# Block maxima of a softmax turned by VectorE in 32x32 blocks and gathered by ScalarE copies, in place of a TensorE transpose

## The chip, the cores and the metric

The kernel runs on one core of one Trainium2 chip. A core has five engines that run side by side and meet only through semaphores: TensorE (PE in the profile, with its weight loads as PEld), VectorE (DVE), ScalarE (ACT), GpSimd (POOL) and SyncE (SP, which only issues DMAs here). The metric is the device time of one execution in microseconds (us), lower is better; the number given for a kernel is the median of several executions.

## What is computed

Two transformer layers over x of 2 batches x 1024 tokens x 512 features, all in float32. In each layer attention and feed-forward both read the same normalised input:

```python
xn = _layernorm(x)
x = x + attention0(xn) + ffn0(xn)      # hidden size 2048
xn = _layernorm(x)
x = x + attention1(xn) + ffn1(xn)      # hidden size 1408, ternary weights with scales
```

Attention has 16 heads of 32 features, rotated queries and keys, and a causal softmax:

```python
scores = einsum('bhqd,bhkd->bhqk', q, k) * 32 ** -0.5
scores = where(causal, scores, lowest)
pattern = softmax(scores, axis=-1)
heads = einsum('bhqk,bhkd->bqhd', pattern, v)
```

The feed-forward part is `down(silu(gate(xn)) * up(xn))`.

## The kernel before, in words

**Stages.** There are four phases, one for each (layer, batch): layer 0 batch 0, layer 0 batch 1, layer 1 batch 0, layer 1 batch 1. In a phase the 16 heads are taken as 4 groups of 4 heads (`HG`), so that 4 heads of 32 features fill 128 partitions. In a group the 1024 queries are taken in 4 blocks of 256 (`QB`). One group and one query block make a `Run`; there are 4 x 4 x 4 = 64 of them. A run with query block `qb` has `qb + 1` steps, each over 256 keys, so a phase has 40 steps and the kernel 160.

**A run.** `scores(n)` computes transposed scores (keys on partitions, queries along the free dimension) with TensorE and lets ScalarE move them to SBUF tile `s`. `blocks(n, h2)` takes maxima with VectorE: a reduction with a built-in transpose gives, for blocks of 32 queries, the maximum over each block of 32 keys; these collect in `rmax`. After the last step one more reduction brings them to `m1`, a tile of 128 partitions x 32: partition 32a + p is query p of its block of 32 as seen by the a-th quarter of the key partitions, and the column is head and query block. What is still missing is the maximum over the four quarters a, which lie on different partitions. `maxima()` does this: it turns `m1`, so that the 32 columns become partitions, and reduces over a to `m2` (32 x 32). `m2` goes to DRAM (`md`), and `spread()` reads it back with a broadcast to all 128 partitions (`mb`). Then `subtract`, `exps`, `summed` (sums of exponentials, on GpSimd and VectorE) and `weighted` (product with the values on TensorE) follow; `weighted` of a step comes `LAG` = 5 steps after its scores.

**Filling.** Between the scores and the weighted sums of a step, TensorE gets other work: feed-forward products, projections, output products (`Fill.run` with its lists). Many of these are written as seven products of half-size blocks, whose results are called `ux`, `uy`, `uz`; `d` is the down product. Their results lie in three PSUM banks (`bank()`, pool `p_m`), which the transpose in `maxima()` uses too.

**Order.** The kernel is not written out in its final order. Every operation is recorded with estimated costs (`Schedule.record`), then a planner (`Schedule.again`) places it: TensorE's pieces keep nearly the recorded order, and each of the other engines takes, among what is ready, what is due first. Each engine then executes its instructions in the planned order, in order, and a waiting instruction holds what stands behind it on its engine. All recorded calls are issued through one helper line (278), so the profile's groups are told apart by tile names and not by lines.

**The place of the change.** When the last step of a run has been recorded (`n == run.steps - 1`), the run is put in the list `found`. `transpose_maxima()` is called before every piece of filling work; it records `maxima()` and `spread()` once the planner's clock says that `m1` is done, or at the latest at the end of the next step's filling, by `transpose_maxima(True)`. `spread_maxima` lets at most two runs hold an `mb` at a time (`rows[0] < 2`).

Of the kernel before, what the change touches and what calls it, by code (L numbers as in the profile page):

```python
# [11 lines left out]
F32 = mybir.dt.float32  # L12
AF = mybir.ActivationFunctionType
ALU = mybir.AluOpType
AX = mybir.AxisListType
# [3 lines left out]
P = 128  # L19
# [6 lines left out]
HG = P // DH  # L26
# [3 lines left out]
SQ = 32  # L30
NSQ = QB // SQ
# [12 lines left out]
def ts(n, size):  # L44
    return slice(n * size, (n + 1) * size)
# [460 lines left out]
def two_layers(ctx: ExitStack, tc: tile.TileContext, x_in, attn_w, ffn_w, ffn_s, rope, out):  # L506
    ctx.enter_context(tc.manual_schedule())
    nc = Schedule(tc.nc)

    def pool(name, bufs, space=None):  # L510
        real = ctx.enter_context(tc.tile_pool(name=name, bufs=bufs, **({"space": space} if space else {})))
        return Pool(real, bufs, {"p_m": "m", "p_av": "av"}.get(name, "other") if space is PSUM else None)
# [20 lines left out]
    small = pool("small", 2)  # L533
# [9 lines left out]
    def bank_free(n):  # L543
        return nc.settled(bank_last[n]) if bank_last[n] else 0.0

    def bank(name, shape=(P, TB), hold=False):
        nc.advance(nc.tensor.free)
        n = min((n for n in range(3) if not bank_held[n]), key=lambda n: (bank_free(n), bank_last[n].first.seq if bank_last[n] else 0))
        bank_held[n] = hold
        t = bank_last[n] = p_m.tile(list(shape), F32, tag=f"m{n}", name=name)  # L550
        if hold:
            bank_of[name] = n
        return t
# [4 lines left out]
    ident = fixed.tile([P, P], F32, tag="ident", name="ident")  # L558
# [633 lines left out]

    waiting, rows = [], [0]

    found = []

    def transpose_maxima(now=False):
        while found and (now or nc.settled(found[0].m1) <= nc.tensor.free):
            found.pop(0).maxima()
            spread_maxima()  # L1200

    def spread_maxima():
        while waiting and rows[0] < 2:
            rows[0] += 1
            waiting.pop(0).spread()

    class Run:
# [69 lines left out]

        def maxima(self):

            tr = bank(f"mtr{self.name}", (HG * NSQ, P))  # L1280
            nc.tensor.transpose(tr, self.m1.rearrange("p h b -> p (h b)"), ident)
            m2 = small.tile([HG * NSQ, SQ], F32, tag="m2", name=f"m2_{self.name}")
            nc.vector.tensor_reduce(m2, tr.rearrange("c (a p) -> c p a", p=SQ), AX.X, ALU.max)
            self.md = dram.tile([HG * NSQ, SQ], F32, tag="md", name=f"md{self.name}")
            nc.sync.dma_start(out=self.md, in_=m2)
            waiting.append(self)
# [124 lines left out]
    now = [0]  # L1411
# [4 lines left out]
    class Fill:  # L1416
# [111 lines left out]
        def run(self, step, share, between=()):  # L1528

            spent = 0.0  # L1530
            while True:

                n = next((i for i, item in enumerate(self.timed) if item[0] <= step), None)
                if n is not None:
                    self.timed.pop(n)[1]()
                    continue
                transpose_maxima()
                chosen = self.choose(step)
                if chosen is None:
                    return spent  # L1540
                fn, cost = chosen
                if spent + cost / 2 > share:
                    return spent
                spent += fn()
                if between:
                    between.pop(0)()
# [124 lines left out]
    def weight(i):  # L1671

        if i >= total + LAG - 6:
            return 1.5
        return 1.2 if i % per_phase < 10 else 1.0
# [3 lines left out]
    for i in range(total + LAG):  # L1679
        ph = min(i // per_phase, len(phases) - 1)  # L1680
        now[0] = i
        if i % per_phase == 0 and i < total:
            while ph not in marks:
                assert fill.run(i - 1, 5.0)
            queue_phase(ph)
        run, n = steps[i] if i < total else (None, 0)
        if run:
            while turned.get((ph, run.g)) != 4:
                assert fill.run(i - 1, 5.0)
            run.scores(n)  # L1690
            if ended and ended.acc:
                ended.total()
        old, m = steps[i - LAG] if i >= LAG else (None, 0)
        if run and n == run.steps - 1:
            run.mask(n)

        if ended:
            ended.normalise()
            ended = None

        def exponentials(r, k, h2, sums=True):
            r.subtract(k, h2)
            r.exps(k, h2)
            if sums:
                r.summed(k, h2)
            if h2 == 1:
                spread_maxima()

        def late(r, k):

            return k == 0 and r.steps == LAG - 1

        between = []
        if old and late(old, m):
            between += [lambda h2=h2: exponentials(old, m, h2) for h2 in range(2)]
        elif old and m == 0:
            for h2 in range(2):
                old.summed(0, h2)
        if run:
            between += [lambda h2=h2: run.blocks(n, h2) for h2 in range(2)]  # L1720
        if 0 <= i - LAG + 1 < total:
            r, k = steps[i - LAG + 1]
            if not late(r, k):

                between += [lambda h2=h2: exponentials(r, k, h2, k > 0) for h2 in range(2)]
        end = total + LAG if ph == len(phases) - 1 else (ph + 1) * per_phase
        share = fill.left((ph + 1) * per_phase) * weight(i) / sum(weight(j) for j in range(i, end))
        goal = share + max(-4.0, min(4.0, carried))
        spent = fill.run(i, goal, between)
        while between:  # L1730
            between.pop(0)()
        transpose_maxima(True)
        if run and n == run.steps - 1:
            found.append(run)
        carried = goal - spent
        if old:
            while (old.ph, 2 * m + 1) not in v:
                spent += fill.run(i, 5.0)
                carried = goal - spent
            tiles = [old.s[m]]  # L1740
            while i < total and spent - goal < 6.0 and max(nc.settled(t) for t in tiles) > nc.tensor.free + SOON:
                more = fill.run(i, 2.0)
                if not more:
                    break
                spent += more
                carried = goal - spent
            old.weighted(m)
            if m == old.steps - 1:
                ended = old

                nc.advance(nc.tensor.free)
                if i + 1 >= total or nc.settled(old.sums) <= nc.tensor.free:
                    old.total()
# [59 lines left out]
```

## Time and profile before

| quantity | value |
|---|---|
| time, median of 3 runs | 1811.73 us (1811.0 to 1814.87) |
| the profiled execution's own time | 1814.8 us |
| its span, first to last instruction | 1812.9 us |
| mean granted TensorE clock | 0.998 |
| PE busy, weight loads | 1798.0 us (99%), 880.0 us (49%) |
| DVE, ACT, POOL busy | 1476.3 (81%), 1041.7 (57%), 1232.6 us (68%) |
| instructions | 25807 |
| DMA | 165.15 MB, 28.5% of 16 engines' span |

Busy shares are averages over the whole span. In the tables of groups, a line gives engine, operation, out<-in by the program's tile names (digits at the end left out, so `m1` and `m2` both read `m`), the shape, how many, the busy time and the mean duration in ns; behind the bar stands the idle time of the engine just before these instructions, and what ended it. In the timeline the first two numbers are the start and the length in us. The end of a matmul is modelled, and the next one can start before it; so time on TensorE is read from start to start.

### The profile page before, as it was taken

The page shows a single profiled execution, that of the slowest core. Times are in us where ns is not written, and L with a number is a line of the kernel's source. Part 1 is how long each engine was busy: PE and PEld are TensorE (multiplying, and loading weights), DVE is VectorE, ACT ScalarE, POOL GpSimd, SP SyncE. Part 2 cuts the span into 40 slices and gives each one's busy share as a digit, 9 for nine tenths or more (in the row PEclk, how much of TensorE's full clock was granted, in tenths as well). Part 3 has the DMA queues.
Part 4 walks back from the last instruction along what each step waited for, and adds up shares of the span by engine and source line. Part 5 has one row for each costly group of instructions (what it writes and reads, how often), then busy time and mean ns, then how long its engine had stood idle before and what let it go on. Part 6 is the DMA issues. An engine that isn't in the chain of part 4 may idle for free.

```text
span 1812.9 us, 25807 instructions
## 1 busy us (share of the span) xinstructions
PE 1798.0 (99%) x9406; PEld 880.0 (49%) x9406; DVE 1476.3 (81%) x1975; ACT 1041.7 (57%) x1240; POOL 1232.6 (68%) x1145
## 2 busy tenths in 40 slices
PE   9999999999999999999999999999999999999998
PEld 5464444444444644444444455444444464444443
DVE  3665988868879668779697798888979998989988
ACT  2444665556546565554575556576565757565762
POOL 6726875956868337446377894886779775866775
PEclk9999999999999999999999999999999999999999
DMA  5324343222232422222133324222223322221211
GB/s 192 99 82 137 114 148 120 67 80 82 80 113 88 138 72 68 70 82 89 56 97 102 115 76 160 76 80 71 77 84 98 125 69 71 70 69 50 67 39 71
DMA packets 140334, 165.15 MB, mean 91 GB/s; under 512 B 13360, under 2 KB 93488, under 8 KB 140208
## 3 DMA queue, kind: packets, MB, share of 16 engines
q1 hardware_dynamic: 140208, 163.50, 28.5%
q8 instruction: 75, 1.23, 0.3%
q14 instruction: 51, 0.42, 0.1%
HBM read 134.62 MB, written 28.84 MB: 90 GB/s over the span
## 4 chain that ended last, share of the span: by engine, by line
PE 89%; POOL 5%; DVE 3%; issue 1%; ACT 1%; DMA 1%; SPq 0%; POOLq 0%; ACTq 0%; DVEq 0%
PE d L278 24%; PE ux L278 19%; PE uy L278 9%; PE sc L278 8%; PE av L278 7%; PE ux_qk L278 5%; PE uz L278 5%; POOL acc L278 2%; PE uy_qk L278 2%; PE ux_v L278 2%; PE uz_qk L278 1%; PE uy_v L278 1%; DVE s L278 1%; PE ps_o L278 1%; PE tr L278 1%
## 5 line engine op out<-in xcount | busy, mean ns | idle before, releaser
L278 POOL TENSOR_TENSOR acc<-acc,s 128x512 f32<-128x512 f32 (+1 forms) x378 | 487.4, 1311 | 84.4 <-ACT s L278 79.9
L278 DVE TENSOR_TENSOR s<-s,mb 128x512 f32<-128x512 f32 (+1 forms) x384 | 489.6, 1300 | 12.5 <-DMA mb<-md 12.5
L278 DVE TRANSPOSE_TENSOR_REDUCE rmax<-s 128x32 f32<-128x1024 f32 (+1 forms) x320 | 351.5, 1117 | 63.9 <-POOL s L278 41.3
L278 PE MATMUL d<-wd,hT 128*128 128x512 f32 x864 | 400.1, 593 | 0.0
L278 ACT ACTIVATE s<-s 128x1024 f32<-128x1024 f32 (+1 forms) x320 | 304.9, 970 | 163.0 <-DVE s L278 161.0
L278 ACT ACTIVATE s<-sc 128x1024 f32<-128x1024 f32 (+1 forms) x320 | 283.3, 934 | 195.1 <-PE sc L278 184.0
L278 POOL TENSOR_TENSOR acc<-s 128x512 f32<-128x512 f32 (+1 forms) x128 | 169.2, 1328 | 195.3 <-ACT s L278 191.5
L278 PEld LDWEIGHTS d<-wd,hT 128*128 128x128 f32 x864 | 161.9, 190 | 192.6 <-issue 186.9
L278 ACT ACT_TABLE_LOAD x167 | 214.3, 1283 | 7.7 <-DVE s L278 4.7
L278 DVE TENSOR_TENSOR x<-d,x 128x512 f32<-128x512 f32 x224 | 151.3, 676 | 75.8 <-PE d L278 75.0
L278 PE MATMUL av<-s,v 128*32 128x256 f32 (+1 forms) x2560 | 159.2, 364 | 0.7 <-ACT s L278 0.5
L278 POOL TENSOR_SCALAR_AFFINE_SELECT s<-s 128x512 f32<-128x512 f32 x128 | 98.9, 784 | 67.0 <-ACT s L278 65.0
L278 PEld LDWEIGHTS av<-s,v 128*32 128x32 f32 x2560 | 67.6, 109 | 145.7 <-issue 97.2
L278 POOL TENSOR_TENSOR hT<-p,hT 128x512 f32<-128x512 f32 x53 | 72.5, 1367 | 77.9 <-ACT hT L278 77.9
L278 PE MATMUL d<-wo,oT 128*128 128x512 f32 x198 | 103.0, 602 | 1.2 <-DVE hT L278 1.2
L278 PE MATMUL ux<-xs,ws 128*128 128x512 f32 x212 | 101.7, 602 | 0.6 <-ACT p L278 0.6
L278 PE MATMUL ux<-xnT,wu 128*128 128x512 f32 x212 | 101.8, 602 | 0.1
L278 PE MATMUL ux<-xnT,wg 128*128 128x512 f32 x212 | 100.9, 598 | 0.4 <-DVE hT L278 0.4
L278 PE MATMUL ux<-xs,wu 128*128 128x512 f32 x212 | 101.2, 600 | 0.0
L278 PE MATMUL uy<-xs,ws 128*128 128x512 f32 x212 | 99.7, 593 | 0.3 <-DVE hT L278 0.3
L278 PE MATMUL uy<-xnT,ws 128*128 128x512 f32 x212 | 99.8, 593 | 0.0
L278 PE MATMUL uz<-xnT,wg 128*128 128x512 f32 x212 | 99.7, 593 | 0.0
(179 smaller groups left out, 2511.2 us busy)
## 6 DMA issues: line engine op xcount, KB each, us to landing
mb<-md SPq DMA_DIRECT2D x64, 512.0 KB, 3.8
wg<-in_gate SPq DMA_DIRECT2D x54, 256.0 KB, 2.9
wd<-in_down SPq DMA_DIRECT2D x32, 256.0 KB, 2.9
xr<-xm SPq DMA_DIRECT2D x32, 256.0 KB, 2.7
wu<-in_up SPq DMA_DIRECT2D x28, 256.0 KB, 3.0
s12gu<-ws SPq DMA_DIRECT2D x26, 256.0 KB, 2.0
ws<-s12gu SPq DMA_DIRECT2D x26, 256.0 KB, 2.6
wd<-wds SPq DMA_DIRECT2D x22, 256.0 KB, 2.9
```

What stands on the lines that cost most here:

```text
L278: target(*[get(a) for a in args], **{k: get(a) for k, a in kwargs.items()})
```

## The change

`maxima()` turns `m1` with VectorE's transpose, which turns each block of 32x32 by itself: quarter a of the result `mt` (32 partitions x 32) is the turned quarter a of `m1`. Four ScalarE copies move the quarters side by side onto the same 32 partitions (`mg`), and VectorE reduces over a as before, now reading SBUF instead of PSUM. No PSUM bank and no TensorE instruction is used. As nothing is placed on TensorE any more, the list `found` and `transpose_maxima` go, and `maxima()` and `spread_maxima()` are recorded at the end of the run's own last step.

```diff
-    found = []
-
-    def transpose_maxima(now=False):
-        while found and (now or nc.settled(found[0].m1) <= nc.tensor.free):
-            found.pop(0).maxima()
-            spread_maxima()
...
         def maxima(self):
-            tr = bank(f"mtr{self.name}", (HG * NSQ, P))
-            nc.tensor.transpose(tr, self.m1.rearrange("p h b -> p (h b)"), ident)
+            mt = small.tile([P, SQ], F32, tag="mt", name=f"mt_{self.name}")
+            nc.vector.transpose(mt, self.m1.rearrange("p h b -> p (h b)"))
+            mg = small.tile([HG * NSQ, P // SQ, SQ], F32, tag="mg", name=f"mg_{self.name}")
+            for a in range(P // SQ):
+                nc.scalar.copy(mg[:, a, :], mt[ts(a, SQ), :])
             m2 = small.tile([HG * NSQ, SQ], F32, tag="m2", name=f"m2_{self.name}")
-            nc.vector.tensor_reduce(m2, tr.rearrange("c (a p) -> c p a", p=SQ), AX.X, ALU.max)
+            nc.vector.tensor_reduce(m2, mg.rearrange("c a s -> c s a"), AX.X, ALU.max)
             self.md = dram.tile([HG * NSQ, SQ], F32, tag="md", name=f"md{self.name}")
             nc.sync.dma_start(out=self.md, in_=m2)
             waiting.append(self)
...
                     self.timed.pop(n)[1]()
                     continue
-                transpose_maxima()
                 chosen = self.choose(step)
...
-        transpose_maxima(True)
         if run and n == run.steps - 1:
-            found.append(run)
+            run.maxima()
+            spread_maxima()
```

## The prediction

> **What bounds the kernel now.** I read the page's busy times first, then who TensorE itself waited for, then the stretches, then the groups that touch the tiles of the change. Sections 1 and 4 of the page:
>
> ```profile
> PE 1798.0 (99%) x9406; PEld 880.0 (49%) x9406; DVE 1476.3 (81%) x1975; ACT 1041.7 (57%) x1240; POOL 1232.6 (68%) x1145
> PE 89%; POOL 5%; DVE 3%; issue 1%; ACT 1%; DMA 1%; SPq 0%; POOLq 0%; ACTq 0%; DVEq 0%
> ```
>
> TensorE has work in all but 14.9 us of the 1812.9 us span, and it carries 89% of the chain that ended last. What it waited for is small; the longest entries of its waits, in us, times and longest:
>
> ```profile
> PE av L278 <- DVE sums L278: 3.1, 7, 1.1
> PE tr L278 <- ACT xn L278: 2.0, 1, 2.0
> PE busy L278 <- POOL rmax L278: 1.4, 1, 1.4
> PE d L278 <- DVE hT L278: 1.2, 1, 1.2
> ```
>
> So nearly every us of the time is a us of TensorE's own sequence, and what counts is what the change takes out of that sequence and what new waits it puts in. Where could a wait arise? By stretches (columns: window and length, busy us and instructions of PE, PEld, DVE, ACT, POOL, clock, DMA):
>
> ```profile
> 1000.00:1500.00 500.00, 495.26 (x2805) 250.39 (x2805) 437.39 (x589) 304.88 (x363) 390.10 (x358) 1.00 0.29 93
> 1500.00:1813.00 313.00, 306.93 (x1751) 140.14 (x1749) 282.57 (x367) 191.75 (x217) 213.24 (x182) 1.00 0.20 62
> ```
>
> From 1000 us on, VectorE is busy 87% and 90% of the time; that is the engine next to TensorE, and PE's one repeated wait (`sums`) is on it. ScalarE stays near 61%.
>
> **What goes from TensorE.** The groups on the tile of the transpose (ns minimum, median, maximum), and two steps of PE's timeline, the first without a transpose, the second with one:
>
> ```profile
> L278 PE MATMUL mtr<-ident,m x64: 272/284/287, 58.2 to 1775.0; 128*32 128x128 f32 x64
> L278 DVE TENSOR_REDUCE m<-mtr x64: 239/272/280, 58.5 to 1775.4; 32x32 f32<-32x128 f32 x64
>   PE mtr L278: 17.9, 19
> ...
> 924.77 0.94 PE L278 MATMUL sc<-q_0T,k_3T 32*128 32x256 f32 x16
> 925.63 1.98 PE L278 MATMUL ux<-xnT,wu 128*128 128x512 f32 x4
> 935.42 1.15 PE L278 MATMUL sc<-q_1T,k_3T 32*128 32x256 f32 x16
> 936.49 0.28 PE L278 MATMUL mtr<-ident,m 128*32 128x128 f32 x1
> 936.61 1.88 PE L278 MATMUL ux<-xs,ws 128*128 128x512 f32 x4
> ```
>
> A transpose's record lasts 0.28 us, but the next product starts 0.12 us after it: the rest overlaps. Read from start to start in the timeline, 41 of the 64 stand behind score or row-sum products and take 0.12 us; 23 stand between other work and take 0.11 us where nothing else holds the next start. The score product ahead of one costs the same with and without it (0.30 us to the next start, for 256 columns), so no change of operand shape is saved. Sum: 41 x 0.12 + 23 x 0.11 = 7.5 us off TensorE. The upper end would be all of the records, 64 x 0.28 = 18 us; I take 7.5, because starts are recorded and ends are not.
>
> Two rules bear on this price. The Trainium skill, "Perfetto Trace Analysis", Identifying the Most-Contended Engine, holds that matmul busy time says little about how full TensorE is and that weight-load busy share is the better measure; here that is 49%, and by it TensorE would have room and the saving could be nothing (1811.7 us). The trace decides otherwise: four 128x512 products start 1.72 us apart, group after group (936.61 above to 938.33), without a gap. "VectorE: DVE Perf Modes", The three transpose paths, gives 390 ns for a TensorE transpose of 128x128 in bf16 and advises TensorE where all 128 partitions must be crossed; at that price 64 would be 25 us, and the time an estimated 1787 us. The 0.12 us from start to start stands against it.
>
> **What VectorE gets.** The reduction of `m2` costs 0.27 us from PSUM and will read SBUF. The nearest rows (busy us, mean ns, idle before):
>
> ```profile
> L278 DVE STREAM_TRANSPOSE rT<-rec 128x256 f32<-128x256 f32 x64 | 28.5, 445 | 2.2
> L278 DVE TENSOR_REDUCE m<-rmax 128x32 f32<-128x128 f32 x16 | 5.8, 360 | 0.3
> L278 DVE RECIPROCAL rec<-av 128x8 f32<-128x8 f32 x64 | 12.4, 194 | 11.3 <-PE av L278 11.0
> L278 ACT COPY p<-ux 128x512 f32<-128x512 f32 x53 | 30.9, 583 | 56.5 <-PE ux L278 49.6 <-POOL q_0T L278 6.7
> L278 ACT COPY raw_k<-ps_k 128x256 f32<-128x256 f32 x2 | 0.7, 372 | 3.3 <-PE ps_k L278 3.3
> ```
>
> The transpose of 32 columns lies between the smallest operation (0.19 us at 8 columns) and `rT` (0.45 us at 256); I take 0.20, near the small row. The reduction of 128 to 32 from SBUF has its own row, 0.36 us. Per run 0.20 + 0.36 - 0.27 = +0.29 us, in 64 runs +18.6 us (ends 18 and 35), to 1495 us or 82%. Against that VectorE stood 17.9 us in 19 runs for the transpose; that goes. From 1000 us on there are 33 runs, so 9.6 us more in 813 us, where 93 us are idle: about 2.8 us of idle time per run cover 0.29 us. If that cover were gone, the cost would be 9.6 us on the path.
>
> **What ScalarE gets.** 64 x 4 = 256 copies of 32x32. Between the two copy rows a column costs (583 - 372) / 256 = 0.82 ns, which leaves 0.16 us at no column, so 0.19 us at 32. Ends: 0.16 us, and 0.30 us, the mean of the smallest ACT operation with pointer operands (`rstd`, 128x4). Sum 49 us (41 to 77), to 1090 us or 60%. The burst of four is 0.75 us in about 28 us. Behind it on ScalarE stand score moves, exponentials and the copies that keep `ux` and `uy`; PE's waits on ScalarE's `p` and `s` are 1.1 us in all today, so I cost the burst at nothing as long as that slack holds. If it did not, each burst would cost at most its 0.75 us, 48 us in all.
>
> **The chain and its waits.** By the timeline, `m2` is done 1.4 to 12.0 us after `m1`, median 6.1; 5.5 of these are the wait for the transpose's turn on TensorE. Now the hops are VectorE, ScalarE, VectorE, each possibly behind work in progress: at least 0.20 + 0.75 + 0.36 = 1.3 us, and with one table load (1.28 us), one exponential (1.06 us) and one subtraction (1.45 us; the means of their groups) ahead, 5.1 us. That is not later than today. `m2`'s reduction is the added wait: on VectorE it holds evictions, subtractions and the next maxima while the copies are under way. The two DMAs per run are the same; on SP's queue the store of `md` still waits for `m2`, with weight loads behind it, and no wait of PE on a DMA stands in the trace. VectorE waited 12.5 us for `mb` in 10 places; an earlier `m2` can only shorten that, and it is worth nothing, since TensorE did not stand behind it. The bank set free can save part of PE's short stalls, and the new order of all lists can add some. PE's 14.9 us without work include about 4 us at the end and the first stalls, so some 7 us could move either way; I count zero.
>
> **The sum.** The profiled execution took 1814.8 us, so it would take 1814.8 - 7.5 = 1807.3 us. It lies 3.1 us above the median of the three runs; against that median the forecast is 1811.7 - 7.5 = 1804.2 us.
>
> **The rivals.** (1) *VectorE becomes the bound in layer 1.* An in-order wait of the `m2` reduction for the four copies, in the 33 runs from 1000 us on, delays `sums` and evictions, and TensorE stands. For: 87 to 90% busy there, and `sums` is already late. Against: 2.8 us idle per run, and one wait of this kind (for PE) goes. The saving is gone at 7.5 / 33 = 0.23 us of standing TensorE per run; from 0.34 us on it is slower beyond measurement. At 0.5 us: 16.5 - 7.5 = +9, 1821 us. (2) *The saving is spent on the order.* With the maxima recorded one step earlier and the banks handed out differently, TensorE's fill work is placed anew, and its waits grow by 4 to 8 us; for it speaks that the waits seen are scattered over many causes, against it that every list is kept as full as before. Middle 6 us: 1810 us. (3) *More than the sum*: freed banks and the earlier `mb` also remove inner waits, or the whole record counted: at most 18 us, 1794 us. That the transposes stay on TensorE can be excluded, as the call is gone.
>
> **How the numbers follow.** Forecast 0.57, rival 1 0.21, rival 2 0.19, rival 3 0.03. About 0.2% (3.6 us) is what a measurement of this kernel can tell from no change: the bounds are 1808.1 and 1815.4 us. Faster is the forecast and rival 3, 0.60; same is rival 2, 0.19; slower is rival 1, 0.21. The forecast's own range is 1799 to 1808 us: up to 5 us of inner waits removed or 4 added. For 8 in 10 it reaches into the start of rival 3 and to rival 1 at some 0.4 us per run (13 - 7.5 = +6): 1797 to 1818 us.
>
> **What would show it.** Right: no `mtr` on PE, PE busy down by 7 to 8 us by starts, VectorE up to about 1495 us, 256 short copies of about 0.19 us, PE's waits still under some 10 us, `m2` done less than 6 us after `m1`. Wrong: waits of PE on `sums`, `hT` or `p` that together pass 7.5 us more than today, above all after 1000 us; a wait of the `m` reduction on ScalarE of more than 1 us per run; copies far above 0.3 us; or TensorE's starts spread wider with no wait named.

## The result, and the profile after

| | before | after |
|---|---|---|
| time, median of 6 runs | 1812.1 us | 1820.31 us (1819.25 to 1822.19) |
| ratio | | 1.0044 [1.0031, 1.0056], 8.0 us slower |
| profiled execution, its span | 1814.8, 1812.9 us | 1820.51, 1818.7 us |
| PE without work in the span | 14.9 us | 25.1 us |

The forecast was 1804.2 us with a range of 1797 to 1818; the change is slower, by a size that is measurable and lies above the range. Sections 1 and 4 of the page of the changed kernel, the busy times and the chain of work that ended last:

```profile
PE 1793.6 (99%) x9342; PEld 876.6 (48%) x9342; DVE 1469.5 (81%) x2039; ACT 1095.6 (60%) x1500; POOL 1223.0 (67%) x1147
PE 87%; DVE 6%; ACT 3%; POOL 2%; issue 1%; DMA 1%; SPq 0%; POOLq 0%; DVEq 0%; ACTq 0%
```

64 instructions are gone from TensorE, and its busy time fell by 4.4 us, from 1798.0 to 1793.6. But the span grew, so the time in which TensorE has no work grew by 10.2 us. The two differ by the 5.8 us between the spans; the rest of the 8.0 us is that the profiled execution of before lay 2.7 us above its median and that of after only 0.2 us. In the chain that ended last, DVE went from 3% to 6%, ACT from 1% to 3%. The longest waits of PE (us, times, longest):

```profile
PE av L278 <- ACT s L278: 4.9, 3, 2.2
PE av L278 <- DVE sums L278: 4.3, 5, 2.0
PE tr L278 <- ACT xn L278: 2.8, 1, 2.8
PE d L278 <- ACT xnT L278: 1.5, 2, 1.2
```

The product with the values, `av`, waited 0.5 us for the exponentials `s` before and 4.9 us now. `sums`, on which the forecast had its eye, added 1.2 us over the whole span; it waits less often and longer. By stretches (columns as before; the first line is the kernel before, the other three the changed one):

```profile
400.00:500.00 100.00, 100.00 (x505) 47.68 (x502) 79.75 (x99) 57.85 (x71) 70.03 (x71) 1.00 0.27 85
400.00:500.00 100.00, 97.21 (x517) 46.16 (x510) 76.31 (x100) 63.34 (x89) 73.32 (x76) 1.00 0.24 77
1000.00:1500.00 500.00, 496.24 (x2758) 249.76 (x2756) 439.80 (x606) 323.37 (x446) 382.23 (x355) 1.00 0.30 94
1500.00:1819.00 319.00, 306.09 (x1776) 141.73 (x1774) 287.57 (x386) 203.41 (x271) 217.84 (x189) 0.99 0.19 61
```

From 1000 to 1500 us, where VectorE is busiest beside a full TensorE, nothing was lost: PE lacks 3.8 us there, 4.7 before. The loss lies in the last stretch, 12.9 us without work against 6.1 before (there PE's waits for `s` and for `sums` are 3.9 and 4.0 us, and were 0.2 and 0.5), and in a place where the forecast did not look at all: from 400 to 500 us in layer 0, where PE had been busy without a gap (100.00) and now lacks 2.8 us. Both are for the most part there too when the new instructions are left out of this order (`a_none` below). The groups of the new tiles (ns minimum, median, maximum; then, in us and times, what ended the idle time ahead of them):

```profile
L278 ACT COPY mg<-mt x256: 200/216/219, 52.5 to 1794.7; 32x32 f32<-32x32 f32 x128
L278 DVE TENSOR_REDUCE m<-mg x64: 326/362/371, 53.4 to 1794.9; 32x32 f32<-32x128 f32 x64
  DVE mt L278: 55.1, 37
  ACT mg L278: 29.1, 37
```

The durations are close to the forecast: 0.216 us a copy (0.19 was taken), 0.36 us a reduction (0.36). ScalarE stands 55.1 us for `mt`, VectorE 29.1 us for `mg`. What such a turn does beside TensorE is seen in the timeline near the end (start and length in us; in brackets the idle time ahead and what ended it):

```profile
1775.69 1.06 ACT L278 ACTIVATE s<-s 128x1024 f32<-128x1024 f32 x1 [2.27 <-DVE s L278]
1776.66 0.88 ACT L278 COPY mg<-mt 32x32 f32<-32x32 f32 x4
1776.67 1.22 DVE L278 TENSOR_TENSOR s<-s,mb 128x1024 f32<-128x1024 f32 x1
1777.44 0.79 ACT L278 ACTIVATE s<-sc 128x768 f32<-128x768 f32 x1
1778.26 1.06 ACT L278 ACTIVATE s<-s 128x1024 f32<-128x1024 f32 x1
1779.37 0.84 PE L278 MATMUL av<-s,v 128*32 128x256 f32 x10 [1.75 <-ACT s L278]
```

The four copies stand between two exponentials. They take 0.88 us, and the exponential behind them (1778.26) is the one that TensorE stands for, 1.75 us. But its subtraction on VectorE is done only at 1776.67 + 1.22 = 1777.89 us, so what stands ahead of it on ScalarE, the copies and a score move, can have held it for 0.37 us. The rest is not theirs: in `a_none`, the same order without the turn, TensorE stands 1.40 us for the same exponential:

```profile
1771.47 1.06 PE L279 MATMUL av<-s,v 128*32 128x256 f32 x12 [1.40 <-ACT s L279]
```

### The profile page after: what moved, and what is told of

Its sections match the earlier page's. It is cut to its first block, busy times and chain, and to the rows that moved or that the text cites. A ratio compares the mean times of both kernels' runs of the same rounds, so it can differ in the third digit from the quotient of the medians.

```text
span 1818.7 us, 26063 instructions
## 1 busy us (share of the span) xinstructions
PE 1793.6 (99%) x9342; PEld 876.6 (48%) x9342; DVE 1469.5 (81%) x2039; ACT 1095.6 (60%) x1500; POOL 1223.0 (67%) x1147
## 4 chain that ended last, share of the span: by engine, by line
PE 87%; DVE 6%; ACT 3%; POOL 2%; issue 1%; DMA 1%; SPq 0%; POOLq 0%; DVEq 0%; ACTq 0%
PE d L278 22%; PE ux L278 18%; PE uy L278 9%; PE sc L278 8%; PE av L278 7%; PE ux_qk L278 6%; PE uz L278 4%; PE ux_v L278 3%; PE uy_qk L278 3%; DVE s L278 2%; PE uy_v L278 2%; PE ps_o L278 1%; PE uz_qk L278 1%; DVE rmax L278 1%; ACT s L278 1%; POOL acc L278 1%
## 5 line engine op out<-in xcount | busy, mean ns | idle before, releaser
L278 DVE TENSOR_TENSOR s<-s,mb 128x512 f32<-128x512 f32 (+1 forms) x384 | 474.3, 1260 | 10.0 <-DMA mb<-md 9.9
L278 POOL TENSOR_SCALAR_AFFINE_SELECT s<-s 128x512 f32<-128x512 f32 x128 | 88.5, 704 | 78.0 <-ACT s L278 76.8
L278 DVE TRANSPOSE_TENSOR_REDUCE sums<-acc 128x16 f32<-128x512 f32 x128 | 87.5, 694 | 27.8 <-POOL acc L278 27.7
```

The costliest lines, as they stand in the source:

```text
L278: target(*[get(a) for a in args], **{k: get(a) for k, a in kwargs.items()})
```

## The experiments

A number behind a label is the ratio to before, with its interval, and the difference of the times. Most of these kernels keep the order of the kernel before and change only what is issued at a place in it: the planner runs on the old operations, and when the instructions are then written out, single ones are left out, replaced or added. So the other instructions of each engine stay in one and the same order. Of each edit only the deciding lines are printed.

**The saving alone.** `e_none` leaves the transpose out and keeps everything else in its place. `m2` is then one VectorE transpose of the first quarter of `m1`; the maximum over the quarters is left out.

```diff
+        for turn, reduce, first_quarter in self.instead:
+            turn.call, reduce.call = (lambda: None), first_quarter
```

> The order of the kernel before on every engine, with the transpose taken off TensorE and nothing put in its place: m2 is made by one VectorE transpose of the first quarter of m1, where the reduction from PSUM stood. The maximum over the four quarters is left out, so the softmax is shifted by another value. It measures the saving alone. The prediction's term: 7.5 us, 1803 to 1805 us. If TensorE is held by something else as soon as it runs ahead (theory B): 1808 us or more.

Measured: 0.9979 [0.9970, 0.9988], 3.8 us faster (2.2 to 5.4). That is half of the 7.5 us of the forecast. (Among executions with a mean granted TensorE clock of 1.000 alone, 10 of 11 here and 18 of 27 of before, the medians are 1808.7 and 1811.7 us, 3.0 us apart.) Where the other half is, PE's timeline of this kernel shows at the place of the transpose that the prediction quotes:

```profile
931.47 1.15 PE L279 MATMUL sc<-q_1T,k_3T 32*128 32x256 f32 x16
932.55 1.98 PE L279 MATMUL ux<-xs,ws 128*128 128x512 f32 x4
934.37 1.88 PE L279 MATMUL uy<-xs,ws 128*128 128x512 f32 x4
```

From the score product to `uy` it takes 934.37 - 931.47 = 2.90 us; before, with the transpose between, it was 938.33 - 935.42 = 2.91 us. The transpose is gone and the time is not: the four `ux` products now take 1.98 us by their record, and took 1.88 behind the transpose. In the prediction's own lines this stood already: `ux` behind a score product without a transpose took 1.98 us. The first full product (`128*128`) after products of 32 rows (`32*128`) takes 0.10 us longer. With the transpose between, this 0.10 us does not show, and the transpose itself takes only 0.12 us to the next start, hardly more than the 0.11 us between full products. So leaving it out saves 0.12 us there and brings back 0.10. Compared place by place over both traces, the 41 places behind score and row-sum products are worth 0.02 us each, 1.0 us in sum, and the other 23 are worth 2.0 us (18 of them 0.11 us; at five the work behind comes hardly earlier): 3.0 us in place of 7.5.

**The turn in the order of before.** `e_order` carries out the whole change in the old order: VectorE's transpose at the place of TensorE's, the copies 0.5 us and the reduction 1.8 us later on the planner's clock. `e_order2` puts VectorE's transpose right behind `m1` and the copies later, so that less is waited for.

```diff
+            turn.call, reduce.call = by_vector, reduced
+            made.append((turn.start + 500.0, turn.seq, gathered))
+            at[reduce] = max(at[reduce], turn.start + 1800.0)
```
```diff
+            turn.call, reduce.call = (lambda: None), reduced
+            copies = max(turn.start, first.start + 2500.0)
+            made.append((first.start + 1.0, first.seq, by_vector))
+            made.append((copies, turn.seq, gathered))
+            at[reduce] = max(at[reduce], copies + 2000.0)
```

> The plan of the kernel before, with every other operation in the place it had there; only the turn is carried out by VectorE's transpose and four ScalarE copies (the copies 0.5 us and the reduction 1.8 us behind the planned start of the transpose on TensorE), and TensorE has no transpose. Theory O (the loss comes from the new order of the lists, not from the new instructions): TensorE is 7.5 us shorter and little is lost, 1803 to 1808 us. Theory W (the engines wait for each other in the turn itself, ScalarE for VectorE and VectorE for the copies, and TensorE's evictions stand behind that): it is as slow as the changed kernel, 1816 to 1824 us.

> As the kernel that carries out the turn by VectorE and ScalarE in the order of the kernel before (1825.6 us), but VectorE's transpose stands right behind m1, the copies not before 2.5 us behind the start of m1, and the reduction 2 us behind the copies, so that ScalarE hardly stands for VectorE nor VectorE for ScalarE (42 us and 18 us there). Theory W (the waits within the turn cost): 1803 to 1812 us. Theory L (ScalarE's load costs, whoever waits): 1818 to 1826 us.

Measured: `e_order` 1.0072 [1.0059, 1.0084], +13.0 us; `e_order2` 1.0040 [1.0027, 1.0052], +7.2 us. The turn alone, in the old order, costs more than it saves. The two differ in the places of the new instructions, and with them in how long the engines stand. The idle time ahead of the new tiles, of `e_order` and then of `e_order2`:

```profile
  DVE mt L1302: 42.1, 22
  ACT mg L1307: 17.7, 13
```
```profile
  DVE mt L1305: 14.8, 7
  ACT mg L1310: 5.8, 5
```

39 us less of standing on two engines that are not the bound go with 5.8 us less time, about 0.15 us for each.

**The load without the waits.** `e_load` keeps the TensorE transpose and adds four copies of a constant on ScalarE at its place, for which nobody waits. `e_vec` adds the VectorE transpose right behind `m1`, unread. `e_vload` adds both.

```diff
+        for first, turn, by_vector, load in self.instead:
+            made.append((first.start + 1.0, first.seq, by_vector))
+            made.append((turn.start, turn.seq, load))
```

> The kernel before with its order and all its instructions, the transpose on TensorE too, and four more ScalarE copies of 32x32 put in at the planned start of each transpose; they read a constant and nothing reads them, so they wait for nobody. ScalarE's load of the change alone, 0.88 us in each of 64 runs. If the load delays ScalarE's evictions and TensorE stands for them (theory L): 1816 to 1824 us. If only the waiting for VectorE costs (theory W): 1811 to 1814 us.

> The kernel before with its order and all its instructions, and one more VectorE transpose of m1 (128x32) right behind m1, which nothing reads. VectorE's load alone, 0.21 us in each of 64 runs. Theory V (VectorE's load is what TensorE feels): 1815 to 1819 us. Theory W (the waits across engines cost, not the load): 1811.5 to 1814 us.

> As the kernel with the extra VectorE transpose, and the four extra ScalarE copies of a constant too: both loads of the change, nobody waiting for anybody, and TensorE's transpose kept. Theory W: some 2 us from ScalarE (1814.2 us with the copies alone) and 1 to 2 from VectorE, 1813.5 to 1816 us; then the remaining 7 us of the kernel with the turn in the order of before (1820.0 us, with 3.4 us saved on TensorE) are waits. Theory V and L together (the loads explain it): 1820 to 1824 us.

Measured: `e_load` 1.0011 [1.0002, 1.0019], +2.0 us; `e_vec` 1.0015 [1.0006, 1.0024], +2.7 us; `e_vload` 1.0028 [1.0016, 1.0041], +5.1 us. The two add up (4.7 against 5.1). So the work itself is not free although both engines have idle time: 256 copies of 0.22 us are 56 us on ScalarE and cost 0.04 us for each; 64 transposes of 0.21 us are 13.4 us on VectorE and cost 0.2 us for each. The costs are close to the bound of measurement one by one, and clear in sum. With them the fixed order is accounted for: -3.8 (saving) + 5.1 (load) leaves 5.9 us of the +7.2 of `e_order2` for its waits, the 0.09 us longer reduction per run and the later `m2`. How these three share it was not measured.

**VectorE alone.** `e_vonly` has VectorE turn the four quarters one by one straight onto the same partitions, with no copy and no engine to wait for.

```diff
+                for a in range(P // SQ):
+                    real.vector.transpose(got["mg"][:, a, :], m1.rearrange("p h b -> p (h b)").real()[ts(a, SQ), :])
```

> In the order of the kernel before, VectorE turns the four quarters of m1 one by one straight onto the same 32 partitions, right behind m1: no TensorE, no ScalarE, no engine waits for another, but VectorE gets some 0.9 us more in each of 64 runs (57 us in all, three times what the change gives it). Theory W: the waits are gone, 1809 to 1814 us. Theory V: VectorE's load costs in proportion, 1822 us or more.

Measured: 1.0056 [1.0044, 1.0069], +10.1 us. In this turn no engine waits for another, and it is no better than `e_order2`. Against `e_none` it is 13.9 us slower; by its page VectorE is busy 1522.5 us, 46.9 us more than in `e_none`. That is 0.3 us of time for each us on VectorE, somewhat more than the 0.2 of `e_vec`.

**A test that failed.** `e_copies` was to be the first test of the load: four copies of a constant recorded in `maxima()`, placed by the planner.

```diff
+            idle = small.tile([HG * NSQ, P // SQ, SQ], F32, tag="mg", name=f"mg_{self.name}")
+            for a in range(P // SQ):
+                nc.scalar.copy(idle[:, a, :], ident[ts(a, SQ), :SQ])
```

> The kernel before with four more ScalarE copies of 32x32 per run, read from a constant and written to a tile that nothing reads: ScalarE's load of the change without its waits. If ScalarE's load is what costs: 1816 to 1822 us. If only the waits cost: 1810 to 1814 us. Theory Z: anything in 1811 to 1825 us, since the plan is another one.

Measured: 1.0278 [1.0264, 1.0292], +50.4 us. It does not measure what was asked. As the copies depend on nothing, the planner put all 256 at the start, as the tile's view shows:

```profile
L278 ACT COPY mg<-ident x256: 200/217/219, 2.1 to 69.6; 32x32 f32<-32x32 f32 x128
```

There they delay the first layer norm, and TensorE stands: it is busy 65.19 of the first 100 us, against 95.78 before. `e_load` was made in its place.

**The place of recording.** `e_place` keeps the TensorE transpose and records the maxima where the change records them, at the end of the run's own last step. `e_engine` does the reverse: the turn of the change, recorded at the old place. The diff is that of `e_place`.

```diff
-                transpose_maxima()
...
-        transpose_maxima(True)
         if run and n == run.steps - 1:
-            found.append(run)
+            run.maxima()
+            spread_maxima()
```

> The kernel before, the turn still on TensorE, but recorded at the end of the run's own last step, as in the changed kernel, and not when the planner's clock has m1 done. The place alone. If the earlier recording does the harm, 1816 to 1824 us, through TensorE waiting for m1. Theories W and C (the new instructions do it): 1810 to 1814 us.

> VectorE's turn and ScalarE's gather as in the changed kernel, but recorded where the kernel before records its maxima. The engines alone. If the earlier place does the harm (as the kernel with the place alone, 1821 us, suggests): 1803 to 1810 us. If the new instructions do harm of their own: 1816 to 1824 us.

Measured: `e_place` 1.0051 [1.0037, 1.0065], +9.2 us; `e_engine` 1.0082 [1.0069, 1.0094], +14.9 us. In `e_place` all 64 transposes stand behind full products, and TensorE waits for `m1` to be there:

```profile
PE mtr L278 <- DVE m L278: 6.7, 7, 2.8
```

6.7 us of waiting, and by an estimate 39 x 0.09 = 3.5 us for the places that had cost 0.02 us behind a score product and cost 0.11 now: 10.2 us, against 9.2 measured. The old place was good for a TensorE transpose, on both counts. For the turn of the change neither place is: with it the old place came out slower than the new one.

**The planner's inputs.** `e_due` gives VectorE's transpose the due time it would have had as a piece of TensorE. `e_costs` gives the planner 0.225 us for a copy, close to their measured distance of 0.228 us; it had reckoned 0.072.

```diff
+        for op, n in self.anchored:
+            piece = next((o for o in self.ops[n:] if o in ideal), None)
+            due[op] = min(due[op], ideal[piece] if piece else due[op])
```
```diff
+        if outs and outs[0].tile.tag == "mg":
+            return 225.0, 225.0
```

> The changed kernel, with one thing put back in the planner: the turn has to be done by the planned start of the TensorE product that is recorded next, as the transpose on TensorE had to. Theory O: the transpose on TensorE was what gave the maxima an early due date; with it back, m1 ends about 6 us after its scores again (10.7 us in the changed kernel, 5.9 us before) and the time falls to 1803 to 1809 us. Theory W: the date changes nothing about the waits in the turn, 1817 to 1823 us. Theory Z (any new plan falls some 5 us to either side): anywhere from 1803 to 1822 us, with m1 early.

> The changed kernel, with the planner's cost of a gather copy set to what the profile shows: 225 ns from copy to copy, where the plan has 72 ns, so that four copies take 0.88 us and not 0.29 us of ScalarE. Theory C (ScalarE runs late against its plan because the copies are under-estimated, and TensorE waits for its evictions): the waits of TensorE on ScalarE (11 us in the changed kernel, 4 us before) go back and the time falls by 4 us or more, to 1810 to 1816 us. Theories O and W: no systematic change, 1816 to 1824 us.

Measured: `e_due` 1.0028 [1.0016, 1.0039], +5.1 us; `e_costs` 1.0059 [1.0046, 1.0071], +10.7 us. Putting the cost of the copies right does not help, so it is not the cause. With the due time the difference to before is 2.9 us smaller than the changed kernel's, but the two intervals overlap (+2.9 to +7.1 and +5.6 to +10.1).

**How much a plan is worth by itself.** Four kernels change one number of the planner that has nothing to do with the maxima: `PORT` 135 to 145 or `RESERVE` 600 to 650, in the kernel before and in the changed one.

```diff
-    PORT = 135.0
+    PORT = 145.0
...
-    RESERVE = 600.0
+    RESERVE = 650.0
```

> The kernel before with one planner constant moved slightly (PORT from 135 to 145 ns), which has nothing to do with the maxima and only gives another plan of the same work. Theory Z (the plan of the kernel before is a lucky one among many; any other plan of the same work costs some us): 1815 to 1825 us. Theory P (the harm comes from what the change does, so a neutral plan costs nothing): 1810 to 1814 us.

> The kernel before with another planner constant moved slightly (RESERVE from 600 to 650 ns), a neutral new plan as the one with PORT at 145 ns (1815.1 us). Theory Z (the plan of the kernel before is a lucky one): again 1813 to 1820 us. Otherwise 1810 to 1812.5 us, and the first one was an accident.

> The changed kernel with the same slight move of that constant (PORT from 135 to 145 ns). Theory Z: the times of the changed kernel scatter too, and its plans are on the whole some 7 us better than those of the kernel before under the same moves: 1808 to 1822 us. Theory P: 1818 to 1822 us, as the changed kernel.

> The changed kernel with a planner constant moved slightly (RESERVE from 600 to 650 ns), a neutral new plan, as was done with the kernel before (no difference). If the changed kernel's plans scatter as widely as the one with PORT at 145 ns says (1828.8 us against 1820.3 us): 1815 to 1830 us. If they scatter no more than those of the kernel before: 1818 to 1824 us.

Measured: before with `PORT` 1.0023 [1.0014, 1.0031], +4.2 us, with `RESERVE` 0.9999 [0.9991, 1.0008], -0.2 us; the changed kernel with `PORT` 1.0093 [1.0078, 1.0109], +16.8 us, with `RESERVE` 1.0058 [1.0045, 1.0070], +10.5 us. A new order alone moves the time by up to 4 us before and up to 9 us after (how much of this is the granted clock is told further down). All of the changed plans (+8.0, +10.5, +16.8, and +5.1, +10.7, +14.9 of the kernels above) are by their medians slower than all with the maxima turned and recorded as before (0, -0.2, +4.2).

**The turn taken out of the changed order.** `a_none` keeps the order of the changed kernel and leaves transpose and copies out, with `m2` as in `e_none`; `d_none` does the same in the order of `e_due`. In both the maximum over the quarters is left out.

```diff
+        for turn, reduce, first_quarter in self.instead:
+            for op in turn:
+                op.call = lambda: None
+            reduce.call = first_quarter
```

> The changed kernel with its order on every engine, but without VectorE's turn and ScalarE's gather; m2 is one VectorE transpose of the first quarter of m1, where the reduction stood. The maximum over the four quarters is left out. It shows how much of the changed kernel's 8 us belongs to the turn itself and how much to the new order. Theory W (load and waits of the turn): 1807 to 1811 us, as with the same work taken out in the order of before (1808.7 us). Theory O (the order): 1815 to 1820 us.

> The order of the kernel with the due date put back (1817.2 us), with its turn left out as in the kernel that took it out of the changed kernel's order (+2.5 us over before): m2 is one VectorE transpose of the first quarter. Theory O (the changed kernel's order is worse because the maxima lost their date): with the date back the order costs nothing, so what is left is TensorE's saving, 1807 to 1810 us. If the date is not what makes the order worse: 1813 to 1816 us, as without it.

Measured: `a_none` 1.0014 [1.0005, 1.0023], +2.5 us; `d_none` 1.0016 [1.0007, 1.0025], +2.6 us. `a_none` and `e_none` issue the same work in two orders: +2.5 against -3.8, so 6.3 us are the order of the changed kernel. The turn itself costs 8.0 - 2.5 = 5.5 us in it. `d_none` shows that the due time of the transpose does not mend the order. The last stretch of `a_none` and PE's waits in it, and below them the same waits of the changed kernel:

```profile
1500.00:1809.26 309.26, 298.73 (x1754) 137.15 (x1752) 277.21 (x366) 190.39 (x214) 214.08 (x184) 1.00 0.20 61
PE av L279 <- DVE sums L279: 3.6, 4, 2.0
PE av L279 <- ACT s L279: 2.8, 2, 1.4
PE av L278 <- DVE sums L278: 4.0, 4, 2.0
PE av L278 <- ACT s L278: 3.9, 2, 2.2
```

Without the turn PE lacks 10.5 us of work there, with it 12.9; from 400 to 500 us it is 1.7 and 2.8 us (`a_none` is busy 98.32 us there). So most of the lost time that the changed kernel's profile shows in these two places comes with the order. Over the whole span PE lacks 14.2 us of work in `e_none`, 19.6 us in `a_none` and 25.1 us in the changed kernel.

**What the granted clock adds.** Each execution has its mean granted TensorE clock on record. It is 1.000 in most executions of the kernel before and in 10 of the 11 of `e_none`; it is 0.997 to 0.999 in all six of the changed kernel. Where it is lost, the profile of the changed kernel shows:

```profile
1792.02 1.12 PE L278 MATMUL d<-wo,oT 128*128 128x512 f32 x2
1797.58 0.63 PE L278 MATMUL av<-s,v 128*32 128x256 f32 x8 [2.15 <-ACT s L278]
1800.47 0.28 PE L278 MATMUL av<-sums,fold 128*32 128x8 f32 x4 [2.05 <-DVE sums L278]
1800.68 2.08 PE L278 MATMUL d<-wo,oT 128*128 128x512 f32 x2
1800.25:1803.66 3.41, 3.19 (x8) 1.62 (x9) 2.96 (x7) 0.43 (x1) 0.00 (x0) 0.50 0.13 40
```

Behind two stalls of TensorE, of 2.15 and 2.05 us, the clock is 0.50 for 3.41 us (the last line is this stretch), and two products that took 1.12 us take 2.08. By an estimate, TensorE loses half of the time that it is busy in such a stretch: 1.6 us here and 1.7 us in another one from 11.66 us on, 3.3 us of this execution. The profiled execution of before lost 3.0 us in the same way, from 8.93 to 15.76 us, while most of its executions, with a clock of 1.000, did not. `p_before_port` was at 0.50 for 10.24 us and TensorE busy for 9.0 of them: 4.5 us, which by this estimate is all of its +4.2 us. Of the 6.3 us of the changed order a part is this too: two executions of `a_none` ran at 1.000 and took 1811.1 and 1811.3 us, about 2.5 us more than `e_none` at 1.000, and the other nine, at 0.996 to 0.999, took 1814.1 to 1819.9 us. In all traces here a stretch at 0.50 within TensorE's work comes behind a stall of TensorE. Not each stall brings one: the profiled execution of `a_none` has a stall of 2.0 us and none. What decides it was not tested.

## Why the prediction was wrong

**Put together.** Half of the 7.5 us was saved (3.8 measured without the turn). The turn in its place gave 5.5 us back, and the order into which the planner put everything gave 6.3 us back: -3.8 + 5.5 + 6.3 = +8.0 us. This is the same three measurements in a row and no check on them; a check of its own is the fixed order, where load alone costs 5.1 us. Of the 6.3 us, about 2.5 are seen at full clock, and the rest goes with stretches at half clock.

**The saving: the step that failed first.** "The score product ahead of one costs the same with and without it (0.30 us to the next start, for 256 columns), so no change of operand shape is saved" looked at the product ahead of the transpose only. The change of shape shows in the product behind, 0.10 us, as soon as no transpose stands between. 41 x 0.12 was mis-sized: these 41 places are worth 0.12 - 0.10 = 0.02 us each. This alone would have left a gain of 3 to 4 us; that the change is slower comes from the two terms that the forecast put at nothing, the load of the turn ("I cost the burst at nothing", "2.8 us of idle time per run cover 0.29 us") and the new order ("I count zero"). The count of places, 0.11 to 0.12 us from start to start, and the choice of starts over the 0.28 us of the record were right.

**ScalarE: durations nearly right, wrong cover.** 49 us were forecast and 256 x 0.216 = 55 us came. "I cost the burst at nothing as long as that slack holds" rested on PE's waits for `p` and `s`, 1.1 us in all. But that these waits are short says how late ScalarE is now, not how early it is: an engine that is just in time also shows no wait. `e_load` put a price on it, 2.0 us. The bound of 48 us that was given for the loss of the cover was far too high.

**VectorE: also not covered.** The 0.29 us per run were counted against 2.8 us of idle time per run. Idle time as a mean does not lie where it is needed: 13.4 us of transposes that nobody reads cost 2.7 us (`e_vec`). The forecast of 1495 us of busy time was wrong the other way: 1469.5 came, though `mt` (0.21 us) and the reduction (0.36) are as forecast, mainly since the 384 subtractions `s<-s,mb` became shorter, in the mean 1260 ns after 1300, 15 of the 25 us. Why was not looked into.

**The waits.** The prediction named the reduction of `m2`, standing for the copies, as the added wait; it is 29.1 us in 37 places. It did not name the one ahead of it: the copies on ScalarE stand for `mt`, 55.1 us in 37 places, and exponentials and score moves stand behind them. That standing has a price is what `e_order` against `e_order2` speaks for, though the new instructions also stand at other places in them. In the changed kernel it stands more than in either and the turn costs 5.5 us, no more than the load alone in the fixed order; so a us of standing has no one price. That it matters where the planner puts the wait is likely, and was not tested by itself.

**The chain held.** `m2` was to be done under 6 us after `m1`: the median is 2.1 us, after 6.1. It was worth nothing, as forecast.

**The rivals.** Rival 1 gave 1821 us and 1820.3 came, but not by its mechanism: VectorE's wait for the copies was to hold TensorE in the 33 runs from 1000 us on. From 1000 to 1500 us PE lost nothing. After 1500 us it stood 4.0 us for `sums` (0.5 before) and 3.9 us for ScalarE's `s` (0.2 before), in six places and not once a run; and without the turn, in `a_none`, it stood 3.6 and 2.8 us there. So these waits belong to rival 2 more than to rival 1. Rival 2, the order, said that TensorE's waits grow by 4 to 8 us: its time without work grew by 5.4 us from `e_none` to `a_none`, and 6.3 us of time were measured. It ended on the side of "no change" only because the 7.5 us stood against it; with the true saving it alone would have made the kernel slower. The two neutral re-plans of before (-0.2 and +4.2 us) could not be known, but that all lists are placed anew was known, and "I count zero" was the step to doubt.

**What stays open.** Why TensorE stands longer in the changed order, and why stretches at half clock follow in it more often. In it `m1` ends on average 10.7 us after the run's last scores, 5.9 before; but `e_due` brings this to 5.1 us, and `d_none` is no better than `a_none`. A part of it may be chance of the planner, whose neutral changes move the changed kernel by up to 9 us. No kernel here with all four quarters in its maximum is faster than the one before beyond the noise; even with nothing in the transpose's place the gain is 3.8 us.

## What to carry to other kernels

Before you count the removal of an instruction as a gain, look at what its neighbour behind it takes with and without it: a change of operand shape may show there only when the instruction between is gone. That an engine is busy 60% and the bound engine hardly ever waits for it does not make further work on it free; ask how early its results come; here each us added cost 0.04 us (ScalarE) to 0.3 us (VectorE). Where an edit makes a planner place everything anew, measure first what a neutral re-plan does, and keep the old order with single instructions replaced to see what the edit itself does. Before a few us are put down to an order, compare executions with the same granted clock.

## What the runs showed of the hardware

Going from products of 32 rows to full ones costs TensorE 0.10 us, visible in the first full product (1.98 us for four in place of 1.88). The Trainium skill, "TensorEngine Tiling (Array Packing)", Key Properties, says that a change of the tiling mode drains TensorE. These runs agree in that the change costs time, 0.10 us; that it is a drain they do not show, and with the small transpose between, the 0.10 us is not seen.

Copies of 32x32 on ScalarE take 0.216 us each but start 0.228 us apart, so that four of them take 0.90 us with no overlap (start and length in us, `x4` the number):

```profile
416.57 0.90 ACT L278 COPY mg<-mt 32x32 f32<-32x32 f32 x4 [3.45 <-DVE mt L278]
```

The Trainium skill, "ScalarE: Activation LUTs", What ACT_TABLE_LOAD costs, gives 186 ns and 0.833 ns per column for an ACTIVATE with immediate scale and bias, by an estimate from it 213 ns for 32 columns; the copies, with 216 ns, agree. It also has ACTIVATEs back to back overlap by about 93 ns, by which four would take an estimated 0.57 us. These copies do not overlap, so the measured distance decides: four cost 0.90 us.
